# Every second sum of the dense weight with its shared low-rank part on ScalarE and GpSimd instead of VectorE, with other planner settings for the last five jobs

## Chip, cores and metric

The kernel runs on one core of a Trainium2 chip. The metric is the device time in microseconds of one execution; of several executions the median is taken. Five compute engines work in parallel, each in its own program order: TensorE (PE, its weight loads shown as PEld), VectorE (DVE), ScalarE (ACT), GpSimd (POOL) and SyncE (SP), which issues nearly all DMAs.

## What is computed

One decoder layer in float32 on `x` of 2 batches x 512 tokens x 1024, with three residual blocks. Cut to what matters, after layernorm in each:

```python
x = x + attn(layernorm(x))    # 32 query heads, 8 key heads; projections with sign(weight), scaled by row
x = x + xattn(layernorm(x))   # rat_read -> causal attention, 16 heads -> rat_write
                              # -> rat_read -> silu(g @ ctx[0].T) * (u @ ctx[1].T) -> rat_write
x = x + ffn(layernorm(x))

def ffn(x, gate, kernel, bias, lora_A, lora_B, lora_A_shared, lora_B_shared):
    base = x @ kernel + bias
    A_eff = einsum('bn,nri->bri', gate, lora_A)        # per batch, rank 32
    B_eff = einsum('bn,nor->bor', gate, lora_B)
    delta = einsum('bor,btr->bto', B_eff, einsum('bri,bti->btr', A_eff, x))
    delta += einsum('or,btr->bto', lora_B_shared, einsum('ri,bti->btr', lora_A_shared, x))
    return base + delta
```

`rat_write` is a per-token state update: a product of `y` with two small matrices gives 376 columns, among them 8 low-rank columns that a second matmul (`du`) spreads to 256; softplus, exponentials and products on 768-wide rows follow, and the hidden state is updated in place. The change lies in `ffn`: the kernel adds the shared low-rank product `lora_A_shared.T @ lora_B_shared.T` to the 1024 x 1024 `kernel` once, and uses the sum as the dense weight.

## The kernel before

**A planner writes the order.** Work is cut into *jobs*, Python generators, one for each stage: `attC` and `attD` (causal attention of batches 0 and 1), `tailW` (weights of the tails), `tailA` and `tailB` (rat_write, rat_read, gates, rat_write of batches 0 and 1), `weights` (`dense_weights`, line 1536), `factorsB` (`factors_back`, line 1519), `denseA` and `denseB` (`dense`, line 1583). A job yields `engine, planned cost, ready time` before each step. `run` (line 453) always takes the step with the smallest planned start plus the *lag* of its job, emits its instructions, and books the cost on the engine. So order on every engine is the planner's, fixed when the program is built; at run time each engine goes through its list and waits where an operand or a buffer is not ready. The lags are settings: one for each job in the list of `build`, and `LAGS` (line 431) for the small side jobs that a job spawns, by name (`weights.joined`, `denseA.stored`, `tailB.gained`). A job in the list also names the jobs that it waits for.

**Helpers.** All vector, scalar and gpsimd instructions are recorded through line 51, all matmuls through line 130, transposes through line 133, loads and stores through line 142. So these four lines stand in nearly all rows of the profile, and groups are told apart by the names of their tiles (`denseA_pair`, `tailB_few`).

**Buffers.** PSUM holds 2 *banks* (128x512 float32) and 3 *pairs* (128x1024). SBUF holds rotating pools: 12 slabs and 4 probs (128x2048), 8 pages (128x1024), 11 rows (128x512), and small tiles. `take` waits for a free buffer, `give` returns it.

**A tail** handles a tile of 128 tokens (`q` = 0 to 3 for each batch; up to three at a time). `write` with the attention output: a 376-column matmul into a bank (4 for write1, 8 for write2), a copy of 8 columns to `few` on VectorE, a transpose of `few` on TensorE, the copy of the 256 `o` columns on ScalarE, two row copies on VectorE, the `du` matmul, then a chain of some 15 VectorE steps with three ScalarE exponentials or logarithms between. `read`: two groups of 4 transposes, 8 matmuls with `read`, and a norm (statistics on VectorE, `rstd` on ScalarE). The gates: two groups of 16 matmuls 128x128 into a pair, with a ScalarE chain and two VectorE products each. Then `write` again and the residual.

**The dense weight.** `dense_weights` loads the shared factors (`shared_A`, `shared_B`) and the bias to pages. For each of four tiles 128 x 4 x 512 of the weight (two in probs, named `weights_probs`, two in slabs, `weights_slab`) it loads the slice of `kernel`, takes two pairs, multiplies the shared factors into them (four matmuls with 32 rows), and spawns two sums: `joined` adds pair `k` to half `k` of the tile, on VectorE:

```python
def joined(w, pair, k, t):
    t = yield "DVE", 1.22, t
    wp = w[:, 2 * k : 2 * k + 2, :]
    nc.vector.tensor_tensor(wp, pair, wp, ALU.add)
    self.give("pair", t)
    return t
```

**The dense product.** For each tile of 128 tokens, `dense` (two at a time) waits for `weights` and `factorsB`, takes layernorm statistics, scales `xs` to a page on VectorE, turns it (two groups of 4 transposes), multiplies it with the batch's low-rank factor (`ranks`, 8 matmuls), reshuffles by one matmul (`eyes`), and accumulates 16 matmuls 128x512 with the four weight tiles into a pair, 8 for each half of the columns; two matmuls with the second factor follow, then the addition of `xs` and the store. The low-rank factors of the batches were made by an earlier job, `factor`, and stored to DRAM; `factorsB` reads them back to two slabs by six loads, 2 MB.

Of the kernel before, what the change touches and what calls it, by code (L numbers as in the profile page):

```python
# [15 lines left out]
ALU = mybir.AluOpType  # L16
AX = mybir.AxisListType

P = 128
# [50 lines left out]
class Kernel:  # L70
# [354 lines left out]
    def output_weights(self):  # L425
# [6 lines left out]
    LAGS = {  # L432
        "added": 0.0, "ahead": 0.0, "attA.ahead": -0.1, "attA.exponentials": -0.1, "attA.finished": 0.3,
        "attB.added": 0.0, "attB.ahead": -0.3, "co.emptied": -0.1, "cv.emptied": -0.1, "denseA.emptied": -1.0,
        "denseA.stored": 1.0, "denseA.summed": -0.6, "denseB.emptied": 0.3, "denseB.stored": -2.0,
        "denseB.summed": -0.1, "emptied": -0.6, "exponentials": 0.3, "factor.put": -1.0, "finished": 0.0,
        "gained": -1.0, "gated": -1.0, "joined": -0.6, "k.scale_of": 0.0, "maxA.reduced": 0.0,
        "maxA.turned": -0.1, "maxB.reduced": 0.3, "maxB.turned": -0.3, "maxD.turned": -0.3, "outA.clean": 1.0,
        "outA.stored": 2.0, "outB.stored": -1.0, "proj0.featured": -1.0, "proj0.valued": -0.6,
        "proj1.featured": -1.0, "proj1.valued": -0.6, "q.scale_of": 0.0, "residual": 1.0, "rotated": 0.0,  # L440
        "stateA.emptied": -0.3, "stateA.rotated": -0.1, "stateB.gained": 0.0, "stateB.rotated": 0.0,
        "stored": 0.6, "summed": -0.6, "tableB.emptied": -2.0, "tailA.gained": -1.0, "tailA.residual": -2.0,
        "tailB.emptied": -0.6, "tailB.gained": -2.0, "tailB.gated": 0.0, "tailB.residual": 0.3,
        "v.scale_of": 0.0, "weights.joined": -0.1, "wo.scale_of": 0.0,
    }
    SPARE = 1

# [168 lines left out]
    def attend(self, groups, operands, scale, causal):  # L618
# [89 lines left out]
        for n, (g, kt) in enumerate(steps):  # L708
# [23 lines left out]
            else:  # L732

                direct = kt == NT - 1 and (g == groups - 1 or self.free["DVE"] > t + self.SPARE)
                if held is not None and not direct:
# [800 lines left out]
    def dense_weights(self):  # L1536
        nc, a = self.io, self.a


        room = yield from self.take("page", 3)  # L1540
        sa = self.page([P, D])
        yield from self.fetch(sa, a["shared_A"], 512, room)
        sbt = self.page([P, D])
        shared = yield from self.fetch(sbt, a["shared_B"], 512, room)
        self.bias = self.page([P, D])
        yield from self.fetch(self.bias, a["bias"].partition_broadcast(P), 512, room)
        self.wk = []
        ends = []

        def joined(w, pair, k, t):  # L1550
            t = yield "DVE", 1.22, t
            wp = w[:, 2 * k : 2 * k + 2, :]
            nc.vector.tensor_tensor(wp, pair, wp, ALU.add)
            self.give("pair", t)
            return t

        for h in range(2):
            for g in range(2):
                cols = slice(h * 512, (h + 1) * 512)
                room = yield from self.take("slab" if h else "probs")  # L1560
                w = (self.slab if h else self.probs)([P, 4, 512])
                src = a["kernel"][g * 512 : (g + 1) * 512, cols].rearrange("(i p) o -> p i o", p=P)
                loaded = yield from self.fetch(w, src, 1024, room)
                room = yield from self.take("pair", 2)
                t = yield "PE", 1.4, max(shared, room)
                pairs = [self.pair() for _ in range(2)]
                for j in range(4):
                    r = slice(32 * j, 32 * j + 32)
                    i = 4 * g + j
                    self.mm(  # L1570
                        pairs[j // 2][:, j % 2, :], lhsT=sa[r, i * P : (i + 1) * P], rhs=sbt[r, cols],
                        start=True, stop=True,
                    )
                for k in range(2):
                    ends.append(self.spawn(joined(w, pairs[k], k, max(t, loaded))))
                self.wk.append(w)
        self.give("page", t, 2)
        return (yield from self.join(*ends))
# [109 lines left out]
    def build(self):  # L1688
        a = self.a
        self.bias = None  # L1690
        self.qkv, self.shifts, self.at, self.x = {}, {}, {}, {}
        self.table, self.norm, self.state, self.left = {}, {}, {}, {}
        self.constants()
        self.exp_and_log()

        self.wscale = self.const([P, 20], "wscale")
        self.load(self.wscale, a["w_scales"])
        self.mean = self.const([P, 20], "mean")
        self.cs = self.const([P, 20], "cs")
        self.cv = self.const([P, H], "cv")  # L1700
        self.co = self.const([P, D], "co")
        self.wkv = self.slab([P, ND, 512], BF16)
        self.wq = [self.slab([P, ND, 512], BF16) for _ in range(2)]
        self.rooms["slab"] = [0.0] * 9
        self.xt = {}
        self.run(
            [
                ("in0", self.split_inputs(0), 0.2),
                ("k", self.weight("k", lambda c: self.wkv[:, :, c * P : (c + 1) * P], 8, 2, 2), 0.2),
                ("v", self.weight("v", lambda c: self.wkv[:, :, H + c * P : H + (c + 1) * P], 10, 2, 2), 1.5),  # L1710
                ("cv", self.scale_rows("v", self.cv, 10, 2), 1.5),
                ("proj0", self.projections(0), 2.0),
                ("q", self.weight("q", lambda c: self.wq[c // 4][:, :, (c % 4) * P : (c % 4 + 1) * P], 0, 8, 2), 1.0),
                ("maxA", self.peaks_1(0), 1.5),
                ("in1", self.split_inputs(1), 1.5),
                ("proj1", self.projections(1), 2.0, "maxA.0"),
                ("wo", self.output_weights(), 1.0, "in1"),
                ("co", self.scale_rows("o", self.co, 12, 8), 1.5),
                ("rot", self.rotations(), 1.5, "attA.2"),
                ("attA", self.attend_1(0, "maxA"), 0.0, "maxA.0"),  # L1720
                ("maxB", self.peaks_1(1), 0.0, "attA.scores"),
                ("outA", self.output_1(0), 0.0, "attA", "wo", "co"),
                ("attB", self.attend_1(1, "maxB"), -1.0, "maxB"),
                ("tableA", self.rotation_table(0), 0.5, "attB.1"),
                ("tableB", self.rotation_table(1), 0.0, "attB.3"),
                ("stateW", self.state_weights(), 3.0, "attB.5"),
                ("outB", self.output_1(1), 0.5, "attB"),
                ("stateA", self.state_inputs(0, True), 0.2, "attB.scores"),
                ("maxC", self.peaks_2(0, "stateA"), 0.5, "stateA"),
                ("stateB", self.state_inputs(1, False), 0.5, "outB"),  # L1730
                ("factor", self.factors(), -0.5, "maxB.3"),
                ("attC", self.attend_2(0, "maxC"), 0.2, "maxC.0"),
                ("factorsB", self.factors_back(), 20.0, "attC"),
                ("maxD", self.peaks_2(1, "stateB"), 0.5, "stateB", "attC.scores"),
                ("tailW", self.tail_weights(), -0.5, "attC", "stateB"),
                ("tailA", self.tails(0), 0.5, "attC", "tailW"),
                ("attD", self.attend_2(1, "maxD"), 0.2, "maxD.1"),
                ("weights", self.dense_weights(), -1.0, "attD"),
                ("tailB", self.tails(1), 0.2, "attD", "tailW", "tailA.1"),
                ("denseA", self.dense_all(0, "tailA"), 0.5, "tailA.0"),  # L1740
                ("denseB", self.dense_all(1, "tailB"), 0.5, "tailB.0"),
            ]
        )
# [104 lines left out]
```

## Time and profile before

| | |
|---|---|
| median of 3 runs | 1129.61 us (1126.38 to 1132.65) |
| the profiled execution | 1127.92 us |
| its span, first to last instruction | 1126.2 us |
| mean granted TensorE clock | 0.960 |
| TensorE busy | 1056.2 us, 94% |
| VectorE busy | 840.2 us, 75% |
| ScalarE busy | 443.9 us, 39% |
| GpSimd busy | 238.2 us, 21% |

The last quarter of the span, by what stands on TensorE in the trace:

| us | work |
|---|---|
| 842 to 859 | the four groups of shared-factor matmuls (`weights_pair`), between the gates of a tail of batch 0 |
| 844 to 862 | the eight sums on VectorE |
| 860 to 872 | write of a tail, reads, turns of the first dense tile |
| 872.5 | first 128x512 matmul of `denseA` |
| to 1122.5 | tails of batch 1 and the eight dense tiles, interleaved |

The loads of `factorsB` are issued from 619.8 us on, the bias at 814.2, the slices of `kernel` from 832.95 to 836.4. How to read it: an engine that is busy less than the span may still be the one that others wait for in a stretch, so the page's shares are read together with tables by stage and with the idle time before single instructions, where the trace names what ended it ("<-DVE tailA_few").

### The profile page before, as it was taken

How to read it: one execution, taken by the hardware profiler on the slowest of the kernel's cores; microseconds unless marked ns; L12 is line 12 of the kernel's file. 1: busy time of each engine (PE TensorE's matmuls, PEld its weight loads, DVE VectorE, ACT ScalarE, POOL GpSimd, SP SyncE). 2: the span in 40 equal slices, each digit the busy share in tenths (PEclk: the TensorE clock that was granted, in tenths of full speed). 3: DMA queues.
4: the chain of work that ended last, by engine and by line, in shares of the span. 5: the costliest groups of instructions: out<-in, count | busy, mean ns of one | idle time of the engine just before them, and what ended most of it. 6: DMA issues, size and time to landing. Idle time of an engine off the chain costs nothing.

```text
span 1126.2 us, 16121 instructions
## 1 busy us (share of the span) xinstructions
PE 1056.2 (94%) x6364; PEld 520.5 (46%) x6364; DVE 840.2 (75%) x1391; ACT 443.9 (39%) x714; POOL 238.2 (21%) x249
## 2 busy tenths in 40 slices
PE   4889999999999998999999899989988999998998
PEld 3554353333233632332554553546455466664643
DVE  8978888578888856787877972499758778687751
ACT  6762101388600214787121256225753233432210
POOL 3542333411321403364452012001210000000000
PEclk8999999999998998999999899969999999987999
DMA  6621000100214221150012200510131101111100
GB/s 255 211 78 29 20 10 20 29 20 23 63 38 145 118 75 38 31 199 1 28 68 74 94 1 1 228 38 1 51 144 50 50 7 57 38 38 38 38 19 38
DMA packets 25520, 70.51 MB, mean 63 GB/s; under 512 B 5330, under 2 KB 5348, under 8 KB 24548
## 3 DMA queue, kind: packets, MB, share of 16 engines
q1 hardware_dynamic: 25444, 69.48, 18.0%
q8 instruction: 50, 0.82, 0.3%
q14 instruction: 26, 0.21, 0.1%
HBM read 50.59 MB, written 10.49 MB: 54 GB/s over the span
## 4 chain that ended last, share of the span: by engine, by line
PE 78%; DVE 13%; ACT 5%; issue 2%; DMA 1%; POOL 1%; SPq 0%; DVEq 0%; ACTq 0%; POOLq 0%
PE proj_bank L130 8%; PE denseA_pair L130 6%; PE denseB_pair L130 5%; PE outA_bank L130 4%; PE attA_pair L130 4%; PE attB_pair L130 4%; PE tailA_bank L130 4%; PE attA_bank L130 3%; PE attB_bank L130 3%; PE maxB_pair L130 3%; PE maxA_pair L130 3%; PE outB_bank L130 3%; PE stateB_bank L130 3%; PE tailB_bank L130 3%; PE factor_bank L130 3%; PE tailA_pair L130 2%
## 5 line engine op out<-in xcount | busy, mean ns | idle before, releaser
L51 DVE TENSOR_REDUCE maxB_mx<-maxB_pair 128x2 f32<-128x1024 f32 x64 | 75.4, 1219 | 21.2 <-PE maxB_pair L130 21.0
L51 DVE TENSOR_REDUCE maxA_mx<-maxA_pair 128x2 f32<-128x1024 f32 x64 | 75.6, 1216 | 14.1 <-PE maxA_pair L130 14.1
L130 PEld LDWEIGHTS <-start_slab 128*128 128x128 bf16 x480 | 45.0, 99 | 69.8 <-issue 22.9
L51 DVE TENSOR_TENSOR attB_probs<-attB_probs,attB_probs 128x1024 f32<-128x1024 f32 x46 | 62.7, 1401 | 12.8 <-PE attB_bank L130 7.1
L51 ACT ACTIVATE attB_probs<-attB_pair 128x1024 f32<-128x1024 f32 x64 | 62.6, 1023 | 20.2 <-PE attB_pair L130 10.1
L51 DVE TENSOR_TENSOR attA_probs<-attA_probs,attA_probs 128x1024 f32<-128x1024 f32 x46 | 56.8, 1283 | 16.8 <-ACT attA_probs L51 9.8
L51 ACT ACTIVATE attA_probs<-attA_pair 128x1024 f32<-128x1024 f32 x64 | 62.0, 1021 | 9.8 <-PE attA_pair L130 9.4
L130 PE MATMUL proj_bank<-in_slab,start_slab 128*128 128x512 bf16 x240 | 57.0, 388 | 1.6 <-ACT in_slab L51 1.6
L130 PE MATMUL proj_bank<-in_probs,start_slab 128*128 128x512 bf16 x240 | 54.7, 380 | 0.0
L130 PE MATMUL maxB_pair<-maxB_row,proj_slab 32*128 32x512 f32 x256 | 47.9, 691 | 3.1 <-DVE maxB_mx L51 3.1
L51 POOL TENSOR_SCALAR proj_row<-proj_row 128x512 f32<-128x512 f32 x24 | 48.1, 2006 | 1.9
L130 PE MATMUL outA_bank<-wo_slab,attA_slab 128*128 128x512 bf16 x192 | 47.6, 398 | 0.7 <-ACT maxB_shift L51 0.7
L130 PE MATMUL attB_pair<-proj_slab,attB_row 32*128 32x512 f32 x256 | 46.9, 686 | 0.0
L51 ACT ACTIVATE proj_row<-proj_bank,cs 128x512 f32<-128x512 f32 x20 | 13.7, 686 | 81.8 <-PE proj_bank L130 61.2
L130 PE MATMUL outB_bank<-wo_slab,attB_slab 128*128 128x512 bf16 x192 | 43.3, 380 | 0.3 <-POOL attB_slab L51 0.3
L130 PE MATMUL attA_pair<-proj_slab,attA_row 32*128 32x512 f32 x256 | 41.6, 639 | 0.3 <-ACT attA_probs L51 0.3
L130 PE MATMUL attB_bank<-attB_probs,proj_slab 128*32 128x512 f32 x256 | 37.6, 619 | 1.1 <-DVE tableA_slab L51 0.7
L51 ACT COPY maxB_shift<-maxB_bank 128x512 bf16<-128x512 bf16 x8 | 4.7, 585 | 85.9 <-PE maxB_bank L133 85.9
L51 POOL TENSOR_SCALAR proj_slab<-proj_row 128x512 f32<-128x512 f32 x24 | 14.8, 616 | 107.7 <-ACT proj_row L51 89.1
L130 PE MATMUL maxA_pair<-maxA_row,proj_slab 32*128 32x512 f32 x256 | 36.8, 640 | 0.0
L51 POOL TENSOR_SCALAR_AFFINE_SELECT attD_probs<-attD_probs 128x512 f32<-128x512 f32 x16 | 12.0, 750 | 114.7 <-ACT attD_probs L51 105.2
L51 POOL TENSOR_SCALAR outA_row<-outA_row 128x512 f32<-128x512 f32 x16 | 21.4, 1340 | 65.0 <-DVE outA_row L51 60.8
(411 smaller groups left out, 2297.3 us busy)
## 6 DMA issues: line engine op xcount, KB each, us to landing
in_page<-in_x_dram SPq DMA_DIRECT2D x8, 512.0 KB, 3.9
q_page<-in_q_weight_dram SPq DMA_DIRECT2D x8, 512.0 KB, 5.4
wo_page<-in_o_weight_dram SPq DMA_DIRECT2D x8, 512.0 KB, 3.6
tailW_slab<-in_write_dram SPq DMA_DIRECT2D x3, 752.0 KB, 10.9
maxA_row<-proj_slab SPq DMA_DIRECT2D x32, 64.0 KB, 2.0
attA_row<-proj_slab SPq DMA_DIRECT2D x32, 64.0 KB, 2.0
maxB_row<-proj_slab SPq DMA_DIRECT2D x32, 64.0 KB, 2.0
outA_page<-in_x_dram SPq DMA_DIRECT2D x4, 512.0 KB, 3.8
```

The lines of the kernel that those rows point to most:

```text
L51: return self.kernel.pin(getattr(self.engine, name)(*args, **kw))
L130: self.pin(self.nc.tensor.matmul(*args, **kw))
```

## The change

For `k = 1`, the second half of each tile, `joined` no longer adds on VectorE. It takes a page, copies the pair to it on ScalarE, gives the pair back, adds page and weight on GpSimd, and gives the page back. For `k = 0` nothing changes. Seven lags and the constant `SPARE` have other values; `factorsB` gets a lag of 3 instead of 20 and waits for `attD` as well as `attC`; `weights` gets a lag of 0.5 instead of -1.0 and waits for `attC` as well.

```diff
     LAGS = {
...
-        "denseA.stored": 1.0, "denseA.summed": -0.6, "denseB.emptied": 0.3, "denseB.stored": -2.0,
-        "denseB.summed": -0.1, "emptied": -0.6, "exponentials": 0.3, "factor.put": -1.0, "finished": 0.0,
+        "denseA.stored": 0.0, "denseA.summed": -0.6, "denseB.emptied": -0.1, "denseB.stored": -2.0,
+        "denseB.summed": 0.0, "emptied": -0.6, "exponentials": 0.3, "factor.put": -1.0, "finished": 0.0,
...
-        "tailB.emptied": -0.6, "tailB.gained": -2.0, "tailB.gated": 0.0, "tailB.residual": 0.3,
-        "v.scale_of": 0.0, "weights.joined": -0.1, "wo.scale_of": 0.0,
+        "tailB.emptied": -0.6, "tailB.gained": -0.6, "tailB.gated": 0.0, "tailB.residual": -0.6,
+        "v.scale_of": 0.0, "weights.joined": 0.0, "wo.scale_of": 0.0,
     }
-    SPARE = 1
+    SPARE = 100
...
         def joined(w, pair, k, t):
+            wp = w[:, 2 * k : 2 * k + 2, :]
+            if k:
+
+                t = max(t, (yield from self.take("page")))
+                t = yield "ACT", 1.0, t
+                part = self.page([P, 2, 512])
+                nc.scalar.copy(part, pair)
+                self.give("pair", t)
+                t = yield "POOL", 2.6, t
+                nc.gpsimd.tensor_tensor(wp, part, wp, ALU.add)
+                self.give("page", t)
+                return t
             t = yield "DVE", 1.22, t
-            wp = w[:, 2 * k : 2 * k + 2, :]
             nc.vector.tensor_tensor(wp, pair, wp, ALU.add)
             self.give("pair", t)
             return t
...
-                ("factorsB", self.factors_back(), 20.0, "attC"),
+                ("factorsB", self.factors_back(), 3.0, "attD", "attC"),
...
-                ("weights", self.dense_weights(), -1.0, "attD"),
+                ("weights", self.dense_weights(), 0.5, "attD", "attC"),
```

## The prediction

> **What bounds the kernel now.** I read the page's busy times and its chain first, then the windows over the last quarter (where the change acts), then the chain and the timelines between 842 and 888 us. Engine, busy us, share of span, instructions:
>
> ```profile
> PE 1056.2 (94%) x6364; PEld 520.5 (46%) x6364; DVE 840.2 (75%) x1391; ACT 443.9 (39%) x714; POOL 238.2 (21%) x249
> ```
>
> TensorE sets the time; a step of another engine costs only where TensorE comes to stand still behind it. By stage (start:end, length, then busy us and count of PE, PEld, DVE, ACT, POOL, then the granted TensorE clock, DMA share, GB/s):
>
> ```profile
> 842.00:868.00 26.00, 22.63 (x146) 15.48 (x145) 22.27 (x37) 9.64 (x21) 0.19 (x1) 1.00 0.26 94
> 868.00:883.00 15.00, 12.89 (x51) 6.28 (x49) 12.50 (x30) 3.78 (x9) 0.19 (x1) 0.89 0.11 36
> 883.00:943.00 60.00, 57.93 (x312) 37.34 (x311) 46.53 (x89) 22.28 (x43) 0.58 (x3) 1.00 0.09 31
> ...
> 982.00:1000.00 18.00, 17.19 (x72) 9.29 (x73) 14.38 (x31) 5.11 (x12) 0.00 (x0) 0.81 0.17 59
> ...
> 1018.00:1040.00 22.00, 19.38 (x79) 10.45 (x80) 16.18 (x38) 5.69 (x13) 0.19 (x1) 0.69 0.13 48
> ```
>
> Where the weights are summed (842 to 862) VectorE is busy 22.27 of 26 us and POOL is empty: the change moves work from the full engine to the empty one. After 868 VectorE is still 83% busy, and TensorE has little slack anywhere; what can be won back is idle time (about 15 us between 842 and the last matmul) and the stages of low clock. The chain in order of time (start, us, what) shows how little separates the sums from the dense product:
>
> ```profile
> 857.44 1.13 PE weights_pair L130 x4
> 858.57 0.00 issue
> 858.57 1.13 PE weights_pair L130 x4
> 859.70 6.16 PE tailA_bank L130 x24
> 865.85 0.02 issue
> 865.88 0.17 DVE tailA_few L51
> ...
> 871.82 0.69 PE denseA_bank L130 x2
> 872.50 5.00 PE denseA_pair L130 x8
> 877.50 2.53 PE tailB_bank L130 x8
> ```
>
> The one thing to hold on to: from 872.5 on TensorE has dense matmuls to fill the time in which VectorE works off the write of tail q2.
>
> **The change, part by part.**
>
> *VectorE loses four sums.* One of the eight lasts 1215 to 1218 ns, so 4 x 1.22 = 4.9 us leave VectorE between 849 and 862. Of TensorE's idle in this stretch only two short waits name a sum (0.37 us at 851.2, 0.73 us at 857.4), so the direct gain is at most 1.1 us; the rest only brings the next chains forward.
>
> *ScalarE gains four copies 128x1024 from PSUM.* Not in the trace in this form; the casts of in_pair with that size take 1001 ns, the exponentials 1023 ns, two 512-wide copies of a bank 2 x 0.59 = 1.17. I take 1.02, so 4.1 us. ScalarE is idle 62% of 842 to 868, but the copies stand in its order: the first behind the o-copy of tail q1 (844.9 in the trace), the next two in a row after q2's o-copy, before tailB's norm and q3's rstd. A rstd held up for 1 us holds up q3's read, which nothing on TensorE needs at once: 0 to 1 us, I take 0.
>
> *POOL gains four additions 128x1024.* Nearest rows: two 128x512 additions of outA_page, 2 x 1307 = 2.61 us; one of 128x1024 to bf16, 2.13 to 2.39. I take 2.5, 10 us in all, finished near 879; the slab halves they complete are read by matmuls after 888, so the additions themselves cost nothing. Only memsets of 0.2 us queue behind them.
>
> *POOL beside VectorE.* One row shows what both at once on SBUF cost. The sums of attB have two SBUF operands; they are 2.36 us for two alone, and beside POOL (VectorE, then POOL; start, us):
>
> ```profile
> 458.88 2.36 DVE L51 TENSOR_TENSOR attB_probs<-attB_probs,attB_probs 128x1024 f32<-128x1024 f32 x2 [0.75 <-PE attB_bank L130]
> 470.30 3.72 DVE L51 TENSOR_TENSOR attB_probs<-attB_probs,attB_probs 128x1024 f32<-128x1024 f32 x2
> ```
> ```profile
> 469.92 1.48 POOL L51 TENSOR_TENSOR attB_slab<-attB_row,attB_slab 128x512 bf16<-128x512 f32 x1
> 471.34 1.60 POOL L51 CAST attB_slab<-attB_row 128x512 bf16<-128x512 f32 x1
> ```
>
> That is 1.36 us more for VectorE in 3.1 us of POOL, or 0.44 per us. On 10 us of POOL the cost is between 0 and 4.4 us of VectorE. About a third of the additions lies where TensorE waits for VectorE, and not all steps there have two SBUF operands; I take 0.7 us, and 4.4 as the upper end.
>
> [...] If every such step of the write chain paid as in the row, the sum would be at the upper end.
>
> *factorsB moved.* Its six loads (2 MB) leave 619.8 us and stand on SP behind the bias load (814.2) and ahead of the kernel loads (832.95). They took 5.7 to 9.1 us to land, so are there by about 830, and their first reader stands after 870; the tailW loads, which they now follow instead of precede, only gain. The kernel loads wait for probs buffers until 833 anyway. Cost 0; if they were issued only with the kernel loads they would add 2 MB, some 9 us by their own row, and would still land before 870.
>
> *The order.* This is what decides. SPARE and the settings that act elsewhere leave TensorE's order untouched up to the second group of weights matmuls (848.7). From there the built order differs: with VectorE's plan lighter, the planner runs q2's write earlier and puts q3's transposes, both `few` turns and the weights groups ahead of denseA q0, whose 16 matmuls now come only after gate 0 of q3. In the trace denseA q0 starts at 872.5. I walked the new order with the durations of the rows:
> - TensorE's `few` turn of q2 waits for a VectorE copy that is queued behind the third sum (1.22) and two 768-wide steps of q1 (0.95 + 0.96). TensorE is through with write and read at 863.6, the copy at 866.5: stall of about 3 us.
> - weights group 4 and write1 of tailB q0 (1.1 + 2.5) end near 870.6. Then its `few` turn waits for a copy that VectorE reaches only after the end of q1's write (2.4), its residual and row copies (1.7), q3's statistics and scaling with rstd on ScalarE (2.4), the fourth sum (1.2) and the statistics of denseA q0 and q1 (2.9): near 877.3. Stall of about 6.7 us, with everything on TensorE queued behind that small turn.
> - Until 888.4 come short pieces (du, transposes, gate 0 of q3, ranks, eyes) of 7 us in 10.9, since each bank waits for its copy.
>
> TensorE's work between 848.7 and 888.4 at full clock, counted in matmul groups: before, 3 weights groups 3.3, gate 3.6, q2's write 5.1, reads 1.7, tailB's write 2.5, turns and du 2.7, ranks and eyes 0.9, and 11.0 of denseA q0's 13.8, some 31 us; after, the same without the dense matmuls but with gate 0 of q3 (3.6) and the extra transposes (0.9), some 24.5. **6.5 us behind.** The stage 868 to 883 already loses 1.65 us to a clock of 0.89; with two longer stalls I put 2.5, so 0.9 more.
>
> *What is won back.* Behind 888 the old order loses about 9 us of idle and 18 x 0.19 + 22 x 0.31 = 10.2 us of clock in the two low stages. In the new order the tail writes fall elsewhere: a thin stretch (near 950, about 4.4 idle and 3.7 of clock), 7.7 of small waits behind it and 1.5 of clock: 17.3 against 19.2, so 2 us back. This is the softest term; I would believe anything from -9 (both low stages gone) to +4.
>
> Sum: -0 for the sums, +6.5 +0.9 +0.7 -2 = **+6.1 us** on the profiled execution of 1127.92 (span 1126.2, 1.7 around it), so 1134.0. That run lies 1.7 below the median of the three runs shown (1129.61; 1126.38 to 1132.65); set against the median the forecast is 1136.
>
> [...]
>
> **The rivals.**
> - *Slower as forecast*, 0.38: dense work pushed behind two stalls, little repaid. 1136.
> - *Contention on top*, 0.08, a worse case of the same sign: VectorE pays 4.4 instead of 0.7, and the clock stays low over the stalls (+3). 1143.
> - *Same*, 0.32: the stalls are real but the dense work put off fills later waits. 6.1 - 5 gives 1130. For it: about 19 us of loss stand behind 888. Against it: those waits are at turns and eyes, where the product before them was already used up.
> - *Faster*, 0.22, the other side, one mechanism: the two low-clock stages. If the denser mix of dense matmuls and tail writes after 943 holds the clock at 1.00, 10.2 us come back and only some 3.7 are lost to the thin stretch; with the early +8.1 and 5 us less idle the time is 1129.6 + 8.1 - 6.5 - 5 - 3 (a shorter second stall) = 1123. It decides from 982 on: with those stages above 0.95 and the second stall under 4 us it wins.
> - *The change does not do what it says*: SPARE moves nothing in the order of the attention additions, and the factorsB move costs nothing by the rows; if the lighter VectorE alone acted, the time would fall by at most the 1.1 us named. That lies inside "same".
>
> **How the numbers follow.** About 0.5% (5.6 us) is what a measurement can tell from no change: slower is above 1135.3, faster below 1124.0. Slower is 0.38 + 0.08 = 0.46, same 0.32, faster 0.22. The range runs from just below the faster rival's 1123 (half of that case lies lower) to the contention rival's 1143, which leaves out some 0.15. The forecast's own range is 1130 to 1141.
>
> **What would show it.** Right: denseA's first 128x512 matmul near 888 instead of 872.5; TensorE idle before the `few` turns of 3 and 6 to 7 us, released by VectorE copies; a clock under 0.9 there; four POOL additions of about 2.5 us. Wrong: second wait under 3 us, or clocks of 1.00 through 982 to 1040, or VectorE steps near the POOL additions at twice their length.

## The result and the profile after

The changed kernel takes 1140.34 us (median of 4 runs, 1139.03 to 1141.88) against 1129.8 (4 runs, 1126.38 to 1132.65): ratio 1.0096, interval 1.0068 to 1.0123. It is slower by about 10.5 us, as forecast in sign; the forecast was 1136 in a range of 1122 to 1143.

The profiled execution took 1141.88 us, span 1140.2. Of its 14 us over the profiled one of before, 3.8 stand ahead of all that the change touches: VectorE's last `attD_slab` step starts at 847.40 instead of 843.63. This mark lay between 843.5 and 848.3 in all profiles shown here, and at 847.0 in one with the old settings, so I do not count it. From the mark to the end it is 292.8 us instead of 282.6, and these 10.2 us are the ones to explain. Engine, busy us, share, instructions:

```profile
PE 1058.4 (93%) x6331; PEld 523.2 (46%) x6364; DVE 840.8 (74%) x1390; ACT 446.9 (39%) x715; POOL 249.0 (22%) x253
```

VectorE's busy time did not fall although four sums of 1.22 us left it; this is the first hint. The windows that answer to those of before (read them some 4 us later):

```profile
842.00:868.00 26.00, 21.85 (x136) 14.91 (x134) 19.94 (x35) 10.96 (x19) 2.49 (x2) 1.00 0.41 149
868.00:883.00 15.00, 8.43 (x29) 4.14 (x25) 14.23 (x20) 5.11 (x8) 5.70 (x4) 0.77 0.01 1
883.00:943.00 60.00, 55.03 (x269) 35.08 (x270) 46.09 (x91) 17.98 (x39) 2.19 (x4) 0.91 0.07 27
...
982.00:1000.00 18.00, 16.65 (x62) 9.69 (x62) 15.60 (x36) 6.95 (x15) 0.00 (x0) 0.93 0.01 1
...
1018.00:1040.00 22.00, 21.82 (x97) 11.18 (x96) 18.59 (x42) 6.63 (x17) 0.20 (x1) 1.00 0.00 1
```

From 868 to 883 TensorE is busy 8.43 of 15 us, 5.55 of that at half clock, while VectorE is busy 14.23. The two low-clock stages of before, 982 and 1018, are nearly gone (0.93 and 1.00 instead of 0.81 and 0.69). TensorE's timeline shows what it waits for (start, us, instruction, idle before it and what ended it):

```profile
872.40 0.38 PE L133 MATMUL tailA_bank<-ident,tailA_few 128*8 128x128 f32 x1 [2.97 <-ACT tailA_row L51]
872.71 2.69 PE L130 MATMUL weights_pair<-weights_page,weights_page 32*128 32x512 f32 x8
875.33 4.08 PE L130 MATMUL tailB_bank<-tailW_slab,attD_slab 128*128 128x376 f32 x8
886.56 0.37 PE L133 MATMUL tailB_bank<-ident,tailB_few 128*8 128x128 f32 x1 [7.16 <-ACT tailB_row L51]
...
899.25 4.13 PE L130 MATMUL denseA_pair<-weights_probs,denseA_page 128*128 128x512 f32 x9
```

The two forecast waits are there, 2.97 and 7.16 us. In the matmuls between them one reads the clock: a weights group that took 1.14 us takes 2.69. The stretches at half clock in this part, as windows (first before, then changed):

```profile
871.81:875.22 3.41, 3.40 (x6) 1.53 (x7) 2.61 (x6) 0.00 (x0) 0.19 (x1) 0.50 0.00 0
```
```profile
871.12:877.95 6.83, 5.55 (x13) 2.60 (x14) 6.76 (x9) 3.34 (x4) 4.55 (x3) 0.50 0.01 2
884.78:895.02 10.24, 7.67 (x29) 6.15 (x30) 7.21 (x18) 4.05 (x12) 0.22 (x2) 0.50 0.04 6
```

The granted clock in them is 0.50. Counted as half of TensorE's busy time there, it costs 1.7 us before and 6.6 in the changed kernel. The first stretch begins at 871.12, when TensorE had stood idle for 1.7 us.

The first 128x512 matmul of `denseA` starts at 899.25 (872.43 before). VectorE's and GpSimd's timelines in the same stretch show what the prediction had undervalued (VectorE before, then VectorE and GpSimd in the changed kernel):

```profile
874.52 0.62 DVE L51 TENSOR_TENSOR tailA_slab<-tailA_slab,tailA_page 128x256 f32<-128x256 f32 x1
...
875.25 1.20 DVE L51 TENSOR_TENSOR tailA_slab<-tailA_slab,tailA_page 128x1024 f32<-128x1024 f32 x1
```
```profile
849.78 2.75 DVE L51 TENSOR_TENSOR tailA_slab<-tailA_slab,tailA_page 128x256 f32<-128x256 f32 x1
...
873.69 2.66 DVE L51 TENSOR_TENSOR tailA_slab<-tailA_slab,tailA_page 128x256 f32<-128x256 f32 x1
...
876.42 3.08 DVE L51 TENSOR_TENSOR tailA_slab<-tailA_slab,tailA_page 128x1024 f32<-128x1024 f32 x1
```
```profile
849.70 2.35 POOL L51 TENSOR_TENSOR weights_probs<-weights_page,weights_probs 128x1024 f32<-128x1024 f32 x1 [12.14 <-ACT weights_page L51]
...
873.40 2.47 POOL L51 TENSOR_TENSOR weights_probs<-weights_page,weights_probs 128x1024 f32<-128x1024 f32 x1 [21.21 <-DVE tailA_page L51]
...
875.97 2.45 POOL L51 TENSOR_TENSOR weights_slab<-weights_page,weights_slab 128x1024 f32<-128x1024 f32 x1
```

These VectorE steps took 0.64, 0.62 and 1.20 us before. Each starts just after a GpSimd addition and ends after it: held 2.11, 2.04 and 1.88 us, together 6.0. The fourth addition (882.32) runs beside a VectorE sum out of PSUM, which keeps its 1.2 us.

**An account by idle time and clock.** I counted, from the `attD_slab` mark to the end, the time in which TensorE had a matmul, with time at half clock counted half (the trace records the clock). This work is 252 to 254 us in every version of the table (257 in e12). What differs is idle time and time at half clock:

| kernel | mark to end | idle | busy at half clock |
|---|---|---|---|
| before | 282.6 | 18.5 | 22.6 |
| changed | 292.8 | 26.3 | 26.2 |
| e1 split, old settings | 280.0 | 21.5 | 11.2 |
| e3 changed, GpSimd 8 columns | 287.4 | 21.6 | 24.2 |
| e5 changed, old weights lag | 285.5 | 21.5 | 22.6 |

These are the profiled executions, which lie some microseconds beside their medians. So of the 10.2 us, 7.8 are idle, 1.8 are clock, and 0.6 lie in the spread of the work. These are net sums. In the first 55 us after the mark the changed kernel loses 8.4 us more idle time and 4.9 more by the clock than before; behind that it loses 3.6 less.

### The profile page after: what moved, and what is told of

Read it like the earlier page. It is cut to its first block, busy times and chain, and to the rows that moved or that the text cites. A ratio compares the mean times of both kernels' runs of the same rounds, so it can differ in the third digit from the quotient of the medians.

```text
span 1140.2 us, 16110 instructions
## 1 busy us (share of the span) xinstructions
PE 1058.4 (93%) x6331; PEld 523.2 (46%) x6364; DVE 840.8 (74%) x1390; ACT 446.9 (39%) x715; POOL 249.0 (22%) x253
## 4 chain that ended last, share of the span: by engine, by line
PE 76%; DVE 13%; ACT 5%; issue 3%; DMA 1%; POOL 1%; SPq 0%; DVEq 0%; ACTq 0%; POOLq 0%
PE proj_bank L130 8%; PE denseB_pair L130 6%; PE denseA_pair L130 5%; PE attA_pair L130 4%; PE attB_pair L130 4%; PE outA_bank L130 4%; PE tailB_bank L130 4%; PE attB_bank L130 3%; PE attA_bank L130 3%; PE maxB_pair L130 3%; PE maxA_pair L130 3%; PE stateB_bank L130 3%; PE outB_bank L130 3%; PE factor_bank L130 3%; PE tailA_bank L130 3%
## 5 line engine op out<-in xcount | busy, mean ns | idle before, releaser
L51 DVE TENSOR_REDUCE maxB_mx<-maxB_pair 128x2 f32<-128x1024 f32 x64 | 75.4, 1218 | 21.6 <-PE maxB_pair L130 21.3
L130 PE MATMUL outA_bank<-wo_slab,attA_slab 128*128 128x512 bf16 x183 | 45.2, 390 | 1.4 <-ACT maxB_shift L51 0.7
```

What stands on the lines that cost most here:

```text
L51: return self.kernel.pin(getattr(self.engine, name)(*args, **kw))
L130: self.pin(self.nc.tensor.matmul(*args, **kw))
```

## The experiments

Theories: (A) the order, with the dense product pushed behind waits of TensorE; (B) GpSimd's additions holding up VectorE where TensorE waits for it. Before each experiment the kernel before was run beside it; its medians were 1128.87 for e1 to e4, 1128.96 for e5 to e8 and 1128.95 for e9 to e12.

**e1, the split alone** (the new `joined` in the kernel before; the settings stay as they were):

```diff
+            if k:
...
+                nc.scalar.copy(part, pair)
...
+                nc.gpsimd.tensor_tensor(wp, part, wp, ALU.add)
```

> Only the split of the sums (ScalarE copy and GpSimd addition for every second half), with all the old settings. In the built order denseA q0's matmuls stay early (right after q2's write, as in the kernel before). If the late dense product (order) carries the loss: 1127 to 1132 us, near the kernel before. If GpSimd's additions holding up VectorE carry it: 1133 to 1137, since four additions of 2.4 us can each hold up a VectorE step by 1.9 to 2.1 us.

1128.66 us, ratio 1.0003 (0.9992 to 1.0015): no difference within some 1.5 us. The split neither helps nor hurts by itself. Its additions also hold a step (VectorE, then GpSimd):

```profile
852.37 2.58 DVE L51 TENSOR_TENSOR tailA_page<-tailA_row,tailA_row 128x256 f32<-128x256 f32 x1
```
```profile
849.27 5.38 POOL L51 TENSOR_TENSOR weights_probs<-weights_page,weights_probs 128x1024 f32<-128x1024 f32 x2 [12.14 <-ACT weights_page L51]
```

but at 852 TensorE has gates (850.41 to 855.7) in its queue and needs nothing of that step.

**e2, the settings alone** (the old `joined` in the changed kernel):

```diff
-            if k:
...
-                nc.scalar.copy(part, pair)
...
-                nc.gpsimd.tensor_tensor(wp, part, wp, ALU.add)
```

> Only the new settings; all eight sums on VectorE as before. Here too the built order keeps denseA q0 early. If the loss needs both parts together (the order): 1127 to 1132 us. If the settings are bad by themselves: 1136 or more.

1143.4 us, ratio 1.0126 (1.0112 to 1.0141). The expectation that the loss needs both parts was wrong: the settings alone cost more than the whole change. They do it by another order: in this trace `denseA`'s first four 128x512 matmuls (887.75) still stand ahead of tailB's `few` turn (889.57), and TensorE waits 7.06 us for the scaled tile `denseA_page`.

**e3, GpSimd's additions cut to 8 columns.**

```diff
-                nc.gpsimd.tensor_tensor(wp, part, wp, ALU.add)
+                nc.gpsimd.tensor_tensor(wp[:, :, :4], part[:, :, :4], wp[:, :, :4], ALU.add)
```

> The changed kernel, but each GpSimd addition covers only 8 of its 1024 columns (the rest of those sums is left out), everything else and the order of all engines unchanged. The three VectorE steps that took 2.7 to 3.1 us beside GpSimd should fall back to 0.64, 0.64 and 1.20 us. If their 6.0 us lie on TensorE's path: 1134 to 1136 us, the wait before tailB's few turn 3 to 4 us instead of 7.2. If the order alone sets the time: 1139 to 1141.

1135.33 us, ratio 1.0059 (1.0040 to 1.0077). The held steps are back at their old lengths, and the second wait is 3.9 us:

```profile
873.00 0.64 DVE L51 TENSOR_TENSOR tailA_slab<-tailA_slab,tailA_page 128x256 f32<-128x256 f32 x1
...
873.77 1.24 DVE L51 TENSOR_TENSOR tailA_slab<-tailA_slab,tailA_page 128x1024 f32<-128x1024 f32 x1
```
```profile
882.04 0.38 PE L133 MATMUL tailB_bank<-ident,tailB_few 128*8 128x128 f32 x1 [3.91 <-ACT tailB_row L51]
```

Against the changed kernel's 1140.34 this is 5.0 us less; each set against the kernel before that ran beside it, 10.5 and 6.5 us of loss, it is 4.1. The intervals of the two ratios overlap a little (1.0068 to 1.0123 and 1.0040 to 1.0077), so the size is rough: 4 to 5 us of the 10.5 go with the hold-ups, about half or more stays without them.

**e4, the changed order with all sums on VectorE.**

```diff
                 t = yield "ACT", 1.0, t
-                part = self.page([P, 2, 512])
-                nc.scalar.copy(part, pair)
+                self.page([P, 2, 512])
...
-                nc.gpsimd.tensor_tensor(wp, part, wp, ALU.add)
+                nc.vector.tensor_tensor(wp, pair, wp, ALU.add)
```

> TensorE's order of the changed kernel, but the four split sums done on VectorE straight from PSUM at the places of the GpSimd additions (no ScalarE copies, no GpSimd additions): 4.9 us more for VectorE, no GpSimd beside it. If the order carries the loss: 1138 to 1142 us, no better than the changed kernel. If GpSimd's hold on VectorE carries it: 1135 to 1137, 4.9 us of sums against 6.0 us of hold-ups, and fewer of them before the few turn.

1139.98 us, ratio 1.0094 (1.0080 to 1.0108), as A expected. Set against e3, 4.9 us more of sums on VectorE cost 4.65 us (1139.98 - 1135.33), where 6.0 us of hold-up cost 4 to 5. This would fit a price of nearly a microsecond of the kernel for a microsecond of VectorE in this order, but it does not show it. In e4 the second wait is shorter (2.82 us), and TensorE stops at another place: in the fourth weights group, behind a sum that the changed kernel does not have on VectorE.

```profile
873.44 2.08 PE L130 MATMUL weights_pair<-weights_page,weights_page 32*128 32x512 f32 x4 [2.07 <-DVE weights_probs L51]
```

**e5, the changed kernel with the old lag of `weights`; e6, the kernel before with the new one.**

```diff
-                ("weights", self.dense_weights(), 0.5, "attD", "attC"),
+                ("weights", self.dense_weights(), -1.0, "attD"),
```

> The changed kernel with one setting put back: the lag of the weights job is -1.0 again (the six other lags, SPARE and the moved factorsB stay). In the built order denseA q0 is early again. If the one lag carries the loss: 1126 to 1131 us, like the split with all the old settings (1128.66). If the small lags have a part in it: 1132 to 1137.

> The kernel before with one setting changed: the lag of the weights job is 0.5. All sums stay on VectorE. If the one lag carries the loss: 1139 to 1145 us, like all new settings without the split (1143.4). If it needs the small lags as well: 1127 to 1133.

e5: 1129.26 us, ratio 1.0003 (0.9985 to 1.0022). With the split, the moved `factorsB`, all six changed entries of `LAGS` and `SPARE` in place, this one line (the lag, and with it the wait for `attC`) brings all of the time back. e6: 1133.79, ratio 1.0048 (1.0031 to 1.0066): the same line alone costs 4.8 us in the kernel before, between the two expectations. There the sums are postponed too (the last VectorE sum of the weights ends at 873.5, before at 862.1), the dense statistics stand behind them, and TensorE waits for the scaled tile:

```profile
877.95 1.12 PE L133 MATMUL denseA_bank<-ident,denseA_page 128*128 128x128 f32 x4 [8.46 <-DVE denseA_page L51]
```

What makes e2 9.6 us slower than e6 was not separated: both have this wait (7.1 and 8.5 us), and the small lags reorder what follows.

**e7, e1 with the edit of e3.**

> The split with the old settings, each GpSimd addition cut to 8 of 1024 columns (the rest of those sums is left out). In the split with old settings one VectorE step was held up beside GpSimd (2.58 instead of 0.41 us) at 852, while TensorE had gates and weights groups to do. If that hold-up is hidden: 1127.5 to 1129.5 us, no change against 1128.66. If GpSimd's price of 5 us holds in this order too: 1123 to 1125.

1129.32 us, ratio 0.9997 (0.9978 to 1.0016). The held step is back at 0.41 us and the time is the same, within some 2.5 us. The hold-up was smaller here (2.2 us against 6.0), so the time alone says little; but in both traces `denseA`'s first 128x512 matmul starts 28.96 us after the mark, with the hold-up (875.93 in e1) as without it (876.82). The price of a hold-up is not a property of the addition but of the place.

**e8, e1 with the lag of `weights` at -2.0.**

```diff
-                ("weights", self.dense_weights(), -1.0, "attD"),
+                ("weights", self.dense_weights(), -2.0, "attD"),
```

> The split with the old settings and the lag of the weights job at -2.0 instead of -1.0: all four weights groups stand in a row ahead of the gates, and denseA q0's first matmul right after q2's gates, earlier than in any kernel so far. If it is the place of the dense product that decides, so that TensorE has matmuls while VectorE works: 1120 to 1127 us. If the groups in a row wait for the sums and the copies (three pairs for eight halves): 1129 to 1133.

1140.48 us, ratio 1.0107 (1.0080 to 1.0133), above both expectations: theory A in its simple form, the earlier the dense product the better, is refuted. Its first matmul came at 872.0, but TensorE's waits show the price: the groups in a row wait for the ScalarE copies,

```profile
PE weights_pair L130 <- ACT weights_page L51: 3.4, 3, 1.2
PE denseA_bank L133 <- DVE denseA_page L51: 3.2, 1, 3.2
```

(total us, times, longest), the gates behind them start 8 us later than before (counted from the mark), and q2's write stands at 887 instead of 860.6, so that the later tails are late too.

**e9, GpSimd's additions in four pieces.**

```diff
-                nc.gpsimd.tensor_tensor(wp, part, wp, ALU.add)
+                for i in range(2):
+                    for c in (slice(0, 256), slice(256, 512)):
+                        nc.gpsimd.tensor_tensor(wp[:, i, c], part[:, i, c], wp[:, i, c], ALU.add)
```

> The changed kernel with each GpSimd addition cut into four of 256 columns; the whole sum is computed. If a VectorE step with two SBUF operands waits for the one GpSimd instruction that is running, it now waits for at most a quarter, about 0.6 us: the three held steps lose 6.0 us down to 2, and the time falls to 1135 to 1138 us. If the hold lasts over all of GpSimd's queue, or the pieces cost GpSimd and VectorE as much: 1139 to 1142.

1140.19 us, ratio 1.0116 (1.0094 to 1.0138), no gain. The three held steps do shrink (VectorE, then GpSimd):

```profile
871.05 1.04 DVE L51 TENSOR_TENSOR tailA_slab<-tailA_slab,tailA_page 128x256 f32<-128x256 f32 x1
...
872.17 1.45 DVE L51 TENSOR_TENSOR tailA_slab<-tailA_slab,tailA_page 128x1024 f32<-128x1024 f32 x1
...
875.50 5.14 DVE L51 TENSOR_SCALAR tailA_row<-tailA_row,tailA_mv,tailA_rstd 128x256 f32<-128x256 f32 x1 [0.60 <-ACT tailA_rstd L51]
```
```profile
875.00 5.49 POOL L51 TENSOR_TENSOR weights_slab<-weights_page,weights_slab 128x256 f32<-128x256 f32 x8
```

With the first one (1.13 us) they lose 1.2 us in all, not 6.0. But now q3's scaling falls beside eight pieces that follow each other without a gap, and the first of its two instructions takes 5.14 us instead of 0.41. The hold-up moved to a later instruction and kept its size. For this one it lasted over all of GpSimd's queue, as the second expectation had it.

**e10, two copies moved forward** (`few` and `o` of tailB's first write, ahead of q3's scaling, the fourth sum and the dense statistics; `early` holds for this write alone); **e11, e10 and e9 together.**

```diff
...
+        if early:
...
+            nc.vector.tensor_copy(few, bank[:, H + 112 : NOUT])
+            nc.scalar.copy(o[:, :H], bank[:, :H])
         first = yield "DVE", 0.2, t
-        few = self.small([P, 8], "few")
-        nc.vector.tensor_copy(few, bank[:, H + 112 : NOUT])
+        if not early:
+            nc.vector.tensor_copy(few, bank[:, H + 112 : NOUT])
         ta = yield "ACT", 0.39, t
-        nc.scalar.copy(o[:, :H], bank[:, :H])
+        if not early:
+            nc.scalar.copy(o[:, :H], bank[:, :H])
```

> The changed kernel with two copies moved and nothing else: the few copy (VectorE) and the o copy (ScalarE) of tailB's first write stand right behind q3's statistics, ahead of q3's scaling, the fourth sum and the statistics of the two dense tiles. The wait of 7.2 us before tailB's few turn should shrink to about 2. If that wait is on the path: 1134 to 1137 us. If what stands behind the turn on TensorE waits for the same VectorE steps anyway: 1139 to 1141.

> Both edits together: the two copies moved and each GpSimd addition in four pieces. If the hold-ups and the place of the copies are two prices on the same path: 1131 to 1134 us, some 6 to 9 below the changed kernel. If they are the same price seen twice: no better than the better of the two.

e10: 1140.85 us, ratio 1.0108 (1.0085 to 1.0131), no gain. The wait moved to the second TensorE instruction behind the turn:

```profile
880.61 0.27 PE L133 MATMUL tailB_bank<-ident,tailB_few 128*8 128x128 f32 x1 [2.27 <-ACT tailB_row L51]
880.81 0.69 PE L130 MATMUL tailA_bank<-tailW_slab,tailA_row 9*128 9x256 f32 x2
885.56 1.19 PE L130 MATMUL tailB_bank<-tailW_slab,tailB_row 9*128 9x256 f32 x2 [4.05 <-DVE tailB_row L51]
```

The du matmul needs a row copy that still stands behind the statistics; a version that moves this copy too was not run. e11: 1137.62 us (1136.79 to 1142.57), ratio 1.0094 (1.0070 to 1.0118), which does not stand clear of the changed kernel's 1.0096. In its trace q3's scaling falls into a gap between GpSimd's pieces and takes its 0.40 us, and the wait before the du matmul is still 3.78 us. Inconclusive, and not the 6 to 9 us expected of two separate prices.

**e12, the changed kernel with the lag of `denseA` at -1.0.**

```diff
-                ("denseA", self.dense_all(0, "tailA"), 0.5, "tailA.0"),
+                ("denseA", self.dense_all(0, "tailA"), -1.0, "tailA.0"),
```

> The changed kernel with the lag of denseA -1.0 instead of 0.5: in the built order the turns, the factor and the 16 matmuls of denseA q0 stand ahead of tailB's few turn, of the gates of q3 and of du. If small turns that block TensorE's queue carry the loss: 1130 to 1136 us. If the work put ahead is then missing further on, as with the weights lag of -2.0 (1140.5): 1138 to 1144.

1185.74 us, ratio 1.0506 (1.0484 to 1.0528). Both sides had the scale wrong. From the mark to the end TensorE is idle 52.8 us and busy at half clock 55.9. TensorE's longest waits are for tails and for dense tiles that VectorE and ScalarE have not come to:

```profile
PE tailA_bank L133 <- ACT tailA_row L51: 10.9, 3, 6.5
PE denseA_bank L133 <- DVE denseA_page L51: 7.6, 3, 6.0
```

## Why the prediction was right, and where it was not

The sign, the two waits and their places came out as forecast. The size did not: 10.5 us where the sum gave 6.1, just inside the upper edge of the forecast's own range (1130 to 1141). Two of the signs that the prediction named for being wrong came, one in full: VectorE steps beside GpSimd's additions took 2.6 to 4.3 times their length; and the clock from 982 to 1040 was near full. The rival "contention on top" (0.08, 1143 us) came nearest, with both of its terms: a larger bill for VectorE (4.4 us; the steps lost 6.0), and some 3 us more for a low clock. No row of before stands behind these 3 us; in the first 55 us after the mark the clock cost 4.9 us more than before, where the sum had 0.9.

*The bound, the copies, the additions, `factorsB`.* All as forecast: copies 1.00 to 1.03 us each (1.02 forecast), additions 2.35 to 2.47 us (2.5), finished at 884.7 with their first reader at 899, and the moved loads cost nothing (e5 has them moved). Four sums less on VectorE gained nothing in e1.

*The stalls.* Found at the forecast places, 2.97 us (3) and 7.16 (6.7). The second agreement is partly luck. The walk reckoned without hold-ups and at full clock; without the hold-ups (e3) the wait is 3.91 us, so some 3.3 of its length go with them, and the rest is shorter than walked because TensorE's matmuls ahead of it ran at half clock (0.50 from 871.12 to 877.95) and came to it later. What ends the wait is the `o` copy of ScalarE, and this copy starts when VectorE's `few` copy has ended, so the prediction's reading, a turn that waits for VectorE's copy, is right in substance:

```profile
886.14 0.37 ACT L51 COPY tailB_row<-tailB_bank 128x256 f32<-128x256 f32 x1 [0.89 <-DVE tailB_few L51]
```

e10 shows that moving these two copies forward is not enough. That it is the whole amount of VectorE work ahead of everything TensorE wants next is the likely reading, and not shown.

*What puts the order there.* The prediction says "with VectorE's plan lighter, the planner runs q2's write earlier". That is wrong. e1 has the lighter plan and keeps `denseA` early, and e6, with all sums on VectorE, has q2's write early by the lag of `weights` alone (12.0 us behind the mark; before 16.9). In the changed kernel this lag, -1.0 to 0.5, decides (e5). It lets other jobs' steps pass, so the last sum of the weights on VectorE ends at 883.2 instead of 862.1, and the dense product, which needs all four tiles by plan, is placed behind it. For the place behind tailB's `few` turn it takes the split as well, since e2 and e6 have `denseA`'s first matmuls ahead of that turn. The walk started from the built order, so its numbers did not depend on the reason. Small slips carry nothing: the 22.27 of 26 us belong to 842 to 868, not 862; ScalarE is idle 63% of that; 1129.6 + 6.1 - 5 is 1130.7.

*The size.* The terms of the sum, against the three profiled executions (in the first three rows the first 55 us after the mark; e3 stands for the changed kernel without hold-ups):

| term | forecast | measured |
|---|---|---|
| order: idle time of TensorE, e3 less before | 6.5 | 3.7 |
| clock around the waits, e3 less before | 0.9 | 3.9 |
| POOL beside VectorE, changed less e3 | 0.7 | 5.7 |
| won back behind | -2 | -3.6 |

Together the measured terms are 9.7; the spread of the counted work makes up the rest of the 10.2. Half-clock stretches differ from one execution to the next (the mean granted clock of the kernel before went from 0.955 to 0.967), so the clock and the last row are rough. Two terms were much too small. The first is "POOL beside VectorE": 0.7 us taken, 4.4 as the upper end; the steps lost 6.0, the profile 5.7, the medians 4 to 5 (e3). The price had been spread as 0.44 us for each microsecond of GpSimd, over the third that lies where TensorE waits. In truth a step was held or not: three steps met an addition, each waited to its end. The first cost TensorE a wait of 1.52 us at 854.07 that e3 does not have, the other two lie before the second wait. The prediction's own row can be read like this too: of its two VectorE steps one took 2.18 us and outlasted the GpSimd addition beside it. The three held steps, with both operands in SBUF, lost 1.88 to 2.11 us each; the sum out of PSUM beside the fourth addition kept its 1.2 us. What holds them is not shown.

The second is the clock: it cost 4.9 us more than before in the changed kernel and 3.9 in e3, where the sum had 0.9. The 0.9 was an estimate from the stage 868 to 883, 1.65 us at a clock of 0.89. That the sum still came within 4.4 us is luck in part: the order was priced 2.8 too high, and more was won back than forecast.

*Behind and won back.* Laying TensorE's work of both traces over each other from the mark on, the changed kernel is about 14 us behind 45 us after it (888 in before), where 8.1 were forecast; without the hold-ups (e3) it is 8.4, against 7.4 forecast without the POOL term. The thin stretch near 950 takes the lag to about 20 at 983, and it falls to about 7 at 1040, where before had its low-clock stages; at the end 10.2 are left. The "faster" rival's premise came true in good part, 0.93 and 1.00 for 0.81 and 0.69, and could not pay for the early loss.

## What to carry to other kernels

Ask of a step that moves to another engine not only what it takes and whether it is hidden, but which instructions of the first engine it will meet: here three steps of the changed kernel and one of e1 that met one were held to its end, by 1.88 to 2.2 us, and the price was nearly full where a third engine waited and not to be seen where it had work queued (4 to 5 us in e3, none in e7, for the same cut). When a change carries settings along, undo them one by one before the mechanism gets the blame or the credit: one line of a planner, put back, undid the whole loss here (e5), though by itself it cost only 4.8 us (e6), and a step to the other side of its old value, in the split with the old settings, cost as much (-2.0, e8). And a wait that shrinks is no gain until the next instruction on the same engine has been looked at.

## What was not expected of the hardware

A VectorE instruction with a single SBUF tensor as operand (and two scalars for each partition) can be held too, and longer; it was seen once. In the profile of e9 the scaling TENSOR_SCALAR 128x256 took 5.14 us instead of 0.41, from inside the first of eight back-to-back GpSimd additions of 0.71 us each until after the last. Sums with two SBUF operands got through beside the pieces in 1.04 to 1.45 us. Cutting GpSimd's work finer helped the one kind and not the other. It also runs the other way: a piece that overlapped the 1.45 us VectorE step took 1.71 us instead of 0.71, and in the profile of before the GpSimd cast of `attB_slab` at 471.34, beside VectorE's sums, took 1.60 us, where the one at 465.94 began with VectorE idle and took 0.61.

The mark at 843 moved by up to 4.8 us between profiles of kernels whose compute engines do the same up to it: some of it in the first 85 us (2 us between before and changed), some in half-clock windows that come in one execution and not in another (645.8 to 652.7 in the changed kernel's profile at 0.50; in the profile of before 640 to 670 is all at 1.00). Two spans alone would have told 14 us where the kernels differ by 10.
